# Nine checks of the adjacency matrix's entries move from VectorE in layer 1 to ScalarE under the joint sums of layers 2 and 3

## The chip, the core and the metric

The kernel runs on one core of a Trainium2 chip. Its engines are TensorE (PE, with its weight loads shown as PEld), VectorE (DVE), ScalarE (ACT), GpSimd (POOL) and SyncE (SP, which here only issues transfers). Each engine works through its own queue of instructions in the order in which the program was written; they meet only in semaphores. The metric is the device time of one execution in microseconds; the runs given here are medians. A clock of 1.00 in the profile's rows is TensorE at full speed.

## The reference

Four graph layers run over x (4096 rows of 64) and an adjacency matrix adj (4096 by 4096, f32). Each layer has the form x = x + layer(relu(layernorm(x)), adj).

```python
# layer 0: attention, masked by adj
att = adj * sigmoid((2 + 2 * (qm @ k.T)) / att_scale + att_bias);  support = att @ h
x = x + support / sqrt(|inner(support)|)
# layer 1: for each row the last 100 neighbours, weights 0.5 ** (their number from the end)
mask = (adj != 0); rank = cumsum(mask, axis=1)
x = x + w @ (h @ weight) + bias
# layer 2
x = x + 1 - 0.1 * h - 0.01 * sum(h * (adj @ h), axis=1)
# layer 3
x = x + relu(concat([h, (adj @ h) / max(deg, 1)]) @ W.T)
```

The entries of adj are drawn as 0 or 1, but nothing in the reference says that they are. The kernel has a fast path that is right only if every entry is 0 or 1, a check of every entry, and a general path that runs after the fast one where any entry is something else.

## The kernel before, in words

**Tiles.** The matrix comes transposed, cut into 8 blocks of 512 rows (ib) and 32 tiles of 128 neighbours (t). The fast path loads it once as fp8 masks, with POOL's transfers converting on the way. It is loaded a second time, in f32, only to be checked. A narrow check takes one tile (128 x 512, 0.25 MB), a wide one two (128 x 1024, 0.5 MB).

**Checks.** `fetch` (L426) issues a load on SP into the next of a ring of buffers, and `check` (L446) lets DVE count the entries that are not 0 or 1, with `(x != 0) != x` and a running sum, into one column of `odd`. A check leaves as many loads under way as `ahead` says: three in layer 1 with three buffers `ckw`, four in the joint sums, where two halves of the area of `s2a` (free once layer 1 is over) make it five buffers. Layer 0 makes 60 narrow checks, layer 1 and the joint sums together 98 wide ones.

**Layer 1** (L1490 to L1610). Masks are counted into ranks by products on PE (`cnt`, L1500), four at a time. Each result goes through a relu that gives the weights `w`, on ACT or on DVE, and the weights enter the sums (`acc`, L1535). Two blocks run together, in four groups and 66 rounds of four. A planner in the program decides which engine converts: `weights` (L1511) keeps a running estimate of when DVE and ACT come free (`Planned`, L53) and takes ACT unless it is late. Checks are paced by `due`, which grows by CHECKS_1 / 66 a round (L1446 and L1587); a check is emitted when one is due and DVE's estimate has room, or when four are due. Five more stand under the counting of the masks ahead of it. At the end of each block its sum is moved out by ACT (`asb`, L243), and `rows1` (L1314) turns it into the inputs of layers 2 and 3: norms on DVE, POOL and ACT, a transpose on PE (`ph`, L1352), its copy by ACT (`ht`, L1357), products on PE (`pn`, L1367), copies by ACT (`fa`, `v`) and a split into two fp16 parts `s` on POOL and DVE.

`rows1` and the like are generators: each `yield` is a place where other work may be emitted. `step` (L374) advances all those under way by one. So the order on every engine is fixed when the program is built.

**Joint sums of layers 2 and 3** (L1697). `both_summed` issues 1024 products of 128 x 256 (L1632), 32 for each of 32 row tiles, two tiles (a pair) at a time. The first six pairs run interleaved over the first 28 neighbour tiles, so that the last blocks of `rows1` have time to finish. After every eight products `beat` (L1615) calls `step`, and on every second beat `check(2)`, which makes 58 wide checks here. When a pair is complete, `last_rows` (L1657) finishes it: `high` on ACT, `agg`, an inner product and `y` on DVE, `xm` on ACT, `y` again on DVE, and a store. The next pair's `h` and `xm` are begun by ACT and POOL shortly before. Seven PSUM banks hold the pairs.

**The flag.** `flagged` (L1287) waits until no check is left, sums `odd` to `bad` on DVE, lets PE add up the partitions (`pf`, L1297) and DVE write a flag. Every engine reads it (L1725) before the last row tile and branches on it at the end.

Of the kernel before, what the change touches and what calls it, by code (L numbers as in the profile page):

```python
# [11 lines left out]
F32 = mybir.dt.float32  # L12
# [13 lines left out]
D = 64  # L26
# [52 lines left out]
def kernel(  # L79
# [35 lines left out]
    nc.vector.memset(one, 1.0)  # L115
    eps = cpool.tile([P, 1], F32, name="eps")
    nc.vector.memset(eps, EPS)
    eps_up = cpool.tile([P, 1], F32, name="eps_up")
    nc.vector.memset(eps_up, EPS / UP / UP)

# [46 lines left out]
    def model(general):  # L167
# [7 lines left out]
        def pool(name, bufs, on=stack, **kw):  # L175
            return on.enter_context(tc.tile_pool(name=name + sfx, bufs=bufs, **kw))
# [1110 lines left out]
        def flagged(flag):  # L1287

            steps = 7 if general else 4
            while checks or fetched:  # L1290
                yield
            bad = small("bad", "")[:, 0:1]
            dve.tensor_reduce(bad, odd, AX.X, ALU.add)
            for _ in range(steps):
                yield
            pf = pm.tile([P, CI], F32, tag="pr", name="pf")
            nc.tensor.matmul(pf[0:1, 0:1], bad, one, start=True, stop=True)  # L1297
            yield
            dve.tensor_scalar(flag, pf[0:1, 0:1], 1.0, None, ALU.min)
# [143 lines left out]

        GROUPS = ((0, 1), (2, 3), (4, 5), (6, 7))
        MOST = 120.0
        PRODUCT, ROUND, CHECKS_1 = 0.216, 1.85, 35  # L1446
        LATEST, CHECK_LATE = (1.8, 2.0, 2.2, 2.0), 1.5
        many, turns = {}, [0]

# [162 lines left out]
        SKEW = 1  # L1612
        summed, beats = [0], [0]

        def beat():  # L1615
            step()
            beats[0] += 1
            if beats[0] % 2:
                check(2)

        flag, any_odd = None, []

        LEAD, SPLIT, PAIR = 6, 28, 2
        BANKS = (2, 5, 6, 0, 1, 3, 4)
# [32 lines left out]
        def last_rows(acc, tiles, tag, begun=None):  # L1657
# [1 line left out]
            n, last = len(tiles), begun is not None  # L1659
            h, xm = begun or rows_begun(tiles, tag)  # L1660
            high, agg = (
                ends.tile([P, n, 2, D], F32, tag=a, name=f"{a}_{tag}", bufs=2)
                for a in ("high", "agg")
            )
            y = ends.tile([P, n, D], F32, tag=f"y{last}", name=f"y_{tag}", bufs=2)
            inn = ends.tile([P, n], F32, tag="inn", name=f"inn_{tag}", bufs=2)
# [65 lines left out]
        if not general:  # L1732
            with tc.manual_schedule():
                for n in range(2):
                    free = q_sb[:, n * NT // 2 : (n + 1) * NT // 2, :]
                    more.append(free.rearrange("p (c a) d -> p c (a d)", c=CG))
                ahead[0], counting[0] = 4, False
                ends = pool("ends", 1, l2)
                both_summed()
            l2.close()  # L1740
            stack.close()
            return any_odd
# [169 lines left out]
```

## Time and profile before

| | us |
|---|---|
| median of 3 runs | 573.25 (572.57 to 573.76) |
| the profiled execution | 572.18, span 569.5 |
| masks counted, then layer 1's rounds | from about 296, rounds from 311.6 |
| last product of layer 1 | starts at 443.86 |
| joint sums, first to last product | 444.08 to 563.3 |
| PE, DVE, ACT, POOL busy | 552.0, 467.5, 358.8, 272.2 |
| wide check on DVE | 1.27 mean |
| conversion of weights, ACT and DVE | 0.61 and 0.69 mean |
| load for a wide check, 0.5 MB, issue to landing | 4.3 median |

A row of the instructions in order of time gives the start, how long it took (several joined rows: from the first start to the last end), the engine, the line in the kernel, the operation with output and input, shapes and a count. A bracket gives the idle time of the engine just before the row and the instruction that ended it. Nearly all rows of DVE and ACT carry L73, the line of the helper that records them, so they are told apart by their tiles. A busy matmul's end is modelled, so a row of products is read by the distance to the next row's start: four products of layer 1 take 0.86 us without a wait, one of the joint sums 0.107. "issue to landing" is the time from SP's issue to the semaphore that says the data is there.

### The profile page before, as it was taken

How to read it: one execution, taken by the hardware profiler on the slowest of the kernel's cores; microseconds unless marked ns; L12 is line 12 of the kernel's file. 1: busy time of each engine (PE TensorE's matmuls, PEld its weight loads, DVE VectorE, ACT ScalarE, POOL GpSimd, SP SyncE). 2: the span in 40 equal slices, each digit the busy share in tenths (PEclk: the TensorE clock that was granted, in tenths of full speed). 3: DMA queues.
4: the chain of work that ended last, by engine and by line, in shares of the span. 5: the costliest groups of instructions: out<-in, count | busy, mean ns of one | idle time of the engine just before them, and what ended most of it. 6: DMA issues, size and time to landing. Idle time of an engine off the chain costs nothing.

```text
span 569.5 us, 9915 instructions
## 1 busy us (share of the span) xinstructions
PE 552.0 (97%) x3368; PEld 280.8 (49%) x3368; DVE 467.5 (82%) x949; ACT 358.8 (63%) x663; POOL 272.2 (48%) x526
## 2 busy tenths in 40 slices
PE   8999999999999999999999999999999999999995
PEld 3563333333333333333334444445454788888884
DVE  4679657799999999898976877778969897799993
ACT  3677667766676776778741888988888432342231
POOL 7624402675757576754444510384634343334332
PEclk9999999999999999999999999999999999999998
DMA  8995952689999999994223465453544788859960
GB/s 145 133 106 47 100 50 20 57 131 154 150 169 150 166 126 173 152 158 121 74 89 113 151 209 168 132 170 112 155 145 132 241 266 304 274 190 323 343 251 21
DMA packets 45612, 87.86 MB, mean 154 GB/s; under 512 B 6272, under 2 KB 24576, under 8 KB 45552
## 3 DMA queue, kind: packets, MB, share of 16 engines
q1 hardware_dynamic: 26112, 69.14, 36.5%
q0 software_dynamic: 18912, 17.77, 33.0%
q8 instruction: 28, 0.46, 0.3%
q10 hardware_dynamic: 528, 0.23, 0.2%
q14 instruction: 32, 0.26, 0.2%
HBM read 135.60 MB, written 1.05 MB: 240 GB/s over the span
## 4 chain that ended last, share of the span: by engine, by line
PE 70%; DVE 13%; POOL 5%; ACT 5%; issue 3%; DMA 2%; DVEq 0%; ACTq 0%; POOLq 0%; SPq 0%
PE acc L1090 15%; PE acc L1632 15%; PE ps L1059 15%; PE acc L1535 8%; PE cnt L1500 8%; PE idle L1183 3%; DVE att L73 3%; DVE ckw L73 2%; PE many L1387 1%; DMA s2a<-adjt_dram 1%; DVE s2a L73 1%; ACT ps L73 1%; DVE rrq L73 1%; POOL mask L211 1%; PE pt L266 1%
## 5 line engine op out<-in xcount | busy, mean ns | idle before, releaser
L1059 PE MATMUL ps<-qt,kt 64*128 64x512 f32 x512 | 123.4, 610 | 3.4 <-DVE att L73 3.0
L1090 PE MATMUL acc<-att,fb 128*64 128x512 f32 x512 | 117.8, 599 | 0.6 <-DVE att L73 0.5
L1632 PE MATMUL acc<-s,mask 128*128 128x256 f16 x1024 | 114.0, 273 | 0.4 <-DVE s L73 0.4
L73 ACT ACTIVATE w<-cnt 128x512 int16<-128x512 f32 x187 | 98.6, 606 | 12.1 <-PE cnt L1500 11.0
L1632 PEld LDWEIGHTS <-mask 128*128 128x128 fp8e4 x1024 | 99.8, 98 | 13.0 <-issue 1.0
L73 DVE TENSOR_TENSOR att<-ps,mask 128x1024 f32<-128x1024 f32 x82 | 98.6, 1217 | 8.6 <-ACT ps L73 8.5
L73 DVE SCALAR_TENSOR_TENSOR ckw<-ckw 128x1024 f32<-128x1024 f32 x76 | 96.0, 1274 | 4.2 <-DMA ckw<-adjt_dram 4.2
L73 ACT ACTIVATE ps<-ps,att_c,att_a 128x1024 f32<-128x1024 f32 x82 | 93.8, 1175 | 1.3 <-PE ps L1059 0.8
L73 ACT ACTIVATE att<-ps,att_c,att_a 128x1024 f32<-128x1024 f32 x46 | 54.6, 1202 | 54.1 <-PE ps L1059 53.9
L1059 PEld LDWEIGHTS ps<-qt,kt 64*128 64x128 f32 x512 | 44.8, 186 | 79.0 <-issue 28.7
L211 POOL DMA_DIRECT2D mask<-adjt_dram x128 | 70.1, 560 | 19.1 <-DMA mask<-adjt_dram 17.4
L73 DVE TENSOR_TENSOR att<-att,mask 128x1024 f32<-128x1024 f32 x46 | 56.9, 1252 | 18.8 <-ACT att L73 18.5
L1500 PE MATMUL cnt<-mask,after 128*128 128x512 fp8e4 x256 | 67.4, 379 | 2.7 <-DVE two L73 0.8
L1090 PEld LDWEIGHTS acc<-att,fb 128*64 128x64 f32 x512 | 33.5, 136 | 73.0 <-issue 67.6
L1535 PE MATMUL acc<-w,s2a 128*128 128x512 bf16 x256 | 66.2, 379 | 1.2 <-ACT asb L73 1.2
L73 DVE TENSOR_SCALAR w<-cnt 128x512 int16<-128x512 f32 x69 | 46.9, 686 | 22.6 <-PE cnt L1500 22.2
L301 POOL TENSOR_TENSOR rs_a<-rs_y 128x4 f32<-128x4 f32 x48 | 19.1, 398 | 67.4 <-DVE rs_y L73 61.0
L73 DVE SCALAR_TENSOR_TENSOR ck<-ck 128x512 f32<-128x512 f32 x60 | 42.8, 713 | 0.0
L1535 PEld LDWEIGHTS <-s2a 128*128 128x128 f16 x256 | 24.6, 98 | 33.6 <-issue 5.6
L1500 PEld LDWEIGHTS <-after 128*128 128x128 bf16 x256 | 24.4, 99 | 31.0 <-issue 2.7
L73 ACT ACTIVATE xm<-xm,inn 128x64 f32<-128x64 f32 x32 | 10.4, 347 | 45.9 <-DVE high L73 44.2
L1183 PE MATMUL idle<-ones 128*128 128x512 bf16 x126 | 30.9, 401 | 1.6 <-DVE ones L73 1.6
(248 smaller groups left out, 611.9 us busy)
## 6 DMA issues: line engine op xcount, KB each, us to landing
ckw<-adjt_dram SPq DMA_DIRECT2D x76, 512.0 KB, 4.3
mask<-adjt_dram POOLq DMA_DIRECT2D x128, 128.0 KB, 8.7
ck<-adjt_dram SPq DMA_DIRECT2D x60, 256.0 KB, 5.9
s2a<-adjt_dram SPq DMA_DIRECT2D x22, 512.0 KB, 4.9
x_sb<-x_dram SPq DMA_DIRECT2D x4, 256.0 KB, 7.5
out_dram<-y POOLq DMA_DIRECT2D x15, 64.0 KB, 3.7
apart_m<-mask SPq DMA_DIRECT2D x16, 16.0 KB, 4.1
mask<-apart_m SPq DMA_DIRECT2D x16, 16.0 KB, 4.3
```

Source lines behind the costliest of these rows:

```text
L73: return op(out, *args, **kw)
L211: nc.gpsimd.dma_start(out=masks[ib][:, g * CG : (g + 1) * CG, :], in_=adjt[ib, g])
L266: nc.tensor.transpose(pt[:, c, :], part, ident)
L301: nc.gpsimd.tensor_tensor(a, y, y, ALU.mult)
L1059: nc.tensor.matmul(ps[:, c, :], kt[half, g, :], qts[ib][half, :], start=True, stop=True)
L1090: nc.tensor.matmul(acc[c * D : (c + 1) * D, :], lhs[:, t, :], rhs[:, c, :], start=(at == 0), stop=(at == NG - 1), skip_group_check=True,)
L1183: nc.tensor.matmul(v.idle[:, v.filling % CG, :], ones, ones.unsqueeze(1).to_broadcast([P, IB // P, P]), start=True, stop=True, skip_group_ ...
L1387: nc.tensor.matmul(pc[q * NT : (q + 1) * NT, :], lane[:, NT - 1 - t : 2 * NT - 1 - t], masks[quad * QUAD + q][:, t, :], start=(t == 0), st ...
L1500: nc.tensor.matmul(cnt, by, what, start=True, stop=True, skip_group_check=True)
L1535: nc.tensor.matmul(accs[ib], apart_s if t < 0 else both(s2a, t), w, start=(t == NT - 1), stop=False, skip_group_check=True,)
L1632: nc.tensor.matmul(acc[:, to, :, :].rearrange("p k d -> p (k d)"), masks[ib][:, t, c * P : (c + 1) * P], s23[:, t, :, :].rearrange("p k d ...
```

## The change

Nine wide checks are handed to ACT. When the joint sums begin, 18 tiles are taken off the end of the list of checks, and a generator `tested_by_act` is advanced by one step on each beat. For each of the nine it issues a load on SP into a buffer of its own (`cka`, one buffer), waits five beats, and makes four passes over the 1024 columns, two beats apart. Each pass sums its results along the row: relu(x - 1) and relu(-x), both zero if every entry lies in 0 to 1, and sign(x) and sign(1 - x), which for 0 and for 1 add up to one and for anything between to two. The load for the next is issued on the beat after the fourth pass. One cycle is 12 beats, so the loads stand at beats 1, 13, ... 97 of 128 and the last pass at beat 108.

`flagged` waits for these too, and `oddness` folds their sums into `bad` with six small steps on DVE. In layer 1 the pace of checks goes from 35 to 26 over the rounds. `agg` goes from two buffers to one. A constant of -1 is filled at the start. By the order of the built instructions, layer 1 then makes 30 wide checks for 40 (those under the counting included), the joint sums 59 on DVE for 58 and 36 passes on ACT, `pf` stands 16 products later on PE, and two conversions of weights move from ACT to DVE; PE's other work, POOL's and the order of ACT's other work stay as they were.

```diff
         def flagged(flag):
             steps = 7 if general else 4
-            while checks or fetched:
+            while checks or fetched or not (general or tested):
                 yield
             bad = small("bad", "")[:, 0:1]
             dve.tensor_reduce(bad, odd, AX.X, ALU.add)
+            if not general:
+                oddness(bad)
...
-        PRODUCT, ROUND, CHECKS_1 = 0.216, 1.85, 35
+        PRODUCT, ROUND, CHECKS_1 = 0.216, 1.85, 26
...
         def beat():
             step()
             beats[0] += 1
             if beats[0] % 2:
                 check(2)
+            next(passes, None)
...
+        BY_ACT, FIRST_PASS = 9, 5
+        tested = []
+
+        def tested_by_act():
+            sums = ends.tile([P, 4, BY_ACT], F32, name="act_sums")
+            unused = evac.tile([P, CG * IB], BF16, tag="asb", name="act_unused", bufs=1)
+            for n in range(BY_ACT):
+                k = by_act.pop() - 1
+                by_act.pop()
+                at = ends.tile([P, CG * IB], F32, tag="cka", name=f"cka_{k}", bufs=1)
+                nc.sync.dma_start(out=at, in_=adjt[k // NT, k % NT // CG].rearrange("p c i -> p (c i)"))
+                for _ in range(FIRST_PASS):
+                    yield
+                for m, (func, bias, scale) in enumerate(
+                    ((AF.Relu, less, 1.0), (AF.Relu, 0.0, -1.0), (AF.Sign, 0.0, 1.0), (AF.Sign, one, -1.0))
+                ):
+                    nc.scalar.activation(
+                        unused, at, func, bias=bias, scale=scale, accum_out=sums[:, m, n : n + 1]
+                    )
+                    yield
+                    if m < 3:
+                        yield
+            tested.append(sums)
+
+        def oddness(bad):
+            out, signs = (small(f"act_{a}", "", ends, 1) for a in ("out", "signs"))
+            sums = tested[0]
+            dve.tensor_reduce(out, sums[:, 0:2, :], AX.XY, ALU.add)
+            dve.tensor_reduce(signs, sums[:, 2:4, :], AX.XY, ALU.add)
+            good = float(BY_ACT * CG * IB)
+            dve.tensor_scalar(out, out, 0.0, None, ALU.not_equal)
+            dve.tensor_scalar(signs, signs, good, None, ALU.not_equal)
+            dve.tensor_tensor(bad, bad, out, ALU.add)
+            dve.tensor_tensor(bad, bad, signs, ALU.add)
...
-                ends.tile([P, n, 2, D], F32, tag=a, name=f"{a}_{tag}", bufs=2)
-                for a in ("high", "agg")
+                ends.tile([P, n, 2, D], F32, tag=a, name=f"{a}_{tag}", bufs=bufs)
+                for a, bufs in (("high", 2), ("agg", 1))
...
                 ends = pool("ends", 1, l2)
+                by_act = [checks.pop() for _ in range(CG * BY_ACT)][::-1]
+                passes = tested_by_act()
                 both_summed()
```

More of the change, by code (lines that the diff above doesn't have):

```diff
@@ L117 @@
     nc.vector.memset(eps, EPS)
+    less = cpool.tile([P, 1], F32, name="less")
+    nc.vector.memset(less, -1.0)
     eps_up = cpool.tile([P, 1], F32, name="eps_up")
@@ L1613, in model @@
         summed, beats = [0], [0]
+        passes = iter(())
         def beat():
```

## The prediction, made before the changed kernel was run

> **What bounds the kernel now.** I read the page's busy row, then the busy time of layer 1 and of the joint sums in stretches of 10 us, then each engine's instructions in order of time at three places.
>
> ```profile
> PE 552.0 (97%) x3368; PEld 280.8 (49%) x3368; DVE 467.5 (82%) x949; ACT 358.8 (63%) x663; POOL 272.2 (48%) x526
> ```
>
> PE is the bound over the span, but stages differ. In the stretches (length, then PE, PEld, DVE, ACT, POOL busy, clock, DMA share, GB/s) 330 to 340 is layer 1, the others the joint sums of layers 2 and 3:
>
> ```profile
> 330.00:340.00 10.00, 10.00 (x48) 4.54 (x47) 7.63 (x13) 9.10 (x19) 0.13 (x1) 1.00 0.58 186
> ...
> 520.00:530.00 10.00, 10.00 (x94) 8.95 (x93) 9.93 (x28) 2.98 (x10) 2.75 (x4) 1.00 0.95 331
> 530.00:540.00 10.00, 10.00 (x94) 8.97 (x92) 9.97 (x24) 1.63 (x6) 4.52 (x6) 1.00 1.01 355
> ```
>
> Layer 1 has ACT as the fuller helper and DMA to spare. In the joint sums ACT is nearly free, but DVE and the DMA engines are both full. The change takes checks out of the first place and puts loads and ACT work into the second.
>
> PE in layer 1 runs four products in 0.86 us, round after round. The exceptions name who made it wait:
>
> ```profile
> 322.05 1.04 PE L1500 MATMUL cnt<-mask,after 128*128 128x512 fp8e4 x4 [0.80 <-DVE two L73]
> ...
> 345.45 0.38 PE L1535 MATMUL acc<-w,s2a 128*128 128x512 bf16 x1 [0.20 <-ACT asb L73]
> ...
> 362.90 1.35 PE L1500 MATMUL cnt<-mask,after 128*128 128x512 fp8e4 x3 [0.36 <-ACT w L73]
> ...
> 429.09 0.59 PE L1500 MATMUL cnt<-mask,after 128*128 128x512 fp8e4 x2 [0.18 <-DVE w L73]
> ```
>
> Only the first and the last end in DVE. The tail of the joint sums, DVE and then PE:
>
> ```profile
> 553.92 1.22 DVE L73 SCALAR_TENSOR_TENSOR ckw<-ckw 128x1024 f32<-128x1024 f32 x1
> 555.06 0.08 DVE L73 DVE_READ_ACCUMULATOR ckw<-ckw 128x1 f32 x1
> 555.18 0.34 DVE L73 TENSOR_REDUCE bad<-odd 128x1 f32<-128x176 f32 x1
> ```
>
> ```profile
> 556.05 0.19 PE L1297 MATMUL pf<-one,bad 128*1 128x1 f32 x2
> 556.17 7.16 PE L1632 MATMUL acc<-s,mask 128*128 128x256 f16 x64
> ```
>
> The product pf stands in PE's own queue. The sum it reads (bad) is ready at 555.52 and PE arrives at 556.05: DVE has 0.53 us to spare, and whatever it is later than that, PE stands still with 64 products to go.
>
> **The change, part by part.**
>
> *Checks out of layer 1.* By the instruction order, layer 1 loses ten wide checks and not nine (40 to 30, those under the counting among them), and the joint sums get 59 on DVE for 58. Ten at 1.15 us from start to next start are 11.5 us of DVE, but PE waits for few of them. Only two of the weights' conversions move from ACT to DVE, so the waits that end in ACT (345, 362, 377, 411) stay. At 322 the check at 319.44 stood right before the two steps PE waited for (320.58, 321.30). One check now stands there where two did, so I take 0.8 of the 0.97 us that PE lost (321.08 to 322.05). At 429 the same check stands in the same place, so its 0.34 us stay. Term: -0.8; bounds 0 and -1.3 (both waits gone).
>
> *Passes at the start of the joint sums.* The first load for ACT (cka) is issued behind a load into s2a's area, and the first pass on it stands on ACT ahead of ht of block 4, which PE needs for its product pn at 452.21.
>
> ```profile
> 450.47 0.42 ACT L73 ACTIVATE s<-fa 128x256 f32<-128x256 f32 x1 [4.61 <-POOL fa L332]
> 450.79 0.35 ACT L73 COPY ht<-ph 128x256 f32<-128x256 f32 x1
> ```
>
> ```profile
> DMA to landing us min/median/max: 8.1/8.1/8.1
> ```
>
> That last line is the load issued at 445.64, the one now just ahead of cka; its neighbours took 5.7 (445.22) and 6.5 us (448.74). PE's last product of layer 1 (443.86, ended 444.24) lets cka out at about 444.2 after the gain above, to land between 449.9 and 452.3. A pass has no row of its own. The nearest are ACT's 1024-column sigmoids, two in 2.26 us and so 1.10 apart, and the 1024-column copy, 1.01. Small passes with an accumulator start 0.24 apart. I take 1.1, between 0.95 and 1.3. So ht ends at 451.4 to 453.8 where pn wants it at 451.5: PE loses 0 to 2.3 us. Behind the waiting pass stand sq of block 6 and the copies and roots of block 5, all feeding later turns of PE; PE already waits 0.5 at 458.08 and 0.4 at 478.57, which would swallow part. Term: +0.7; bounds -0.9 (DVE's lead removes those two waits) and +2.6.
>
> *SP's queue.* Each cka waits for the fourth pass on the one before, since there is one buffer, and DVE's own loads queue behind it. On DVE's side four loads are out at a time, so a hold of 2 us costs nothing while they last. But ACT's lateness is handed on: the first load's last two passes follow the root kept (455.35 now, about 457.5 behind late copies) and end at 460; the second load lands at 465 and its last pass follows the root rs of block 7 (472.37 now, 473.6 then), ending at 474.7; the third lands at 480 and its last pass follows the copies of block 7 (481.82 to 482.6 now, 484.2 then), ending at 485.3. That puts the load of cka_248 at 485.4, to land at 489.8 (4.4 to 4.8 us there). Its first pass stands ahead of h and high of pair 0 (1.02 us), so DVE's agg of that pair starts at about 492 instead of 489.32, and all DVE's checks behind it are as late. DVE has 3.4 us of waits for stores (DMA out_dram) before 510 that may take some back. Term: +1.2; bounds 0 and +2.6.
>
> *Passes under a full DVE.* From 515 on DVE runs 6.25 us a pair (agg at 540.27 and 546.53) with no gap, PE 6.83 (64 products of 0.107), so DVE catches up 0.58 a pair. Loads land in 5.2 to 5.4 us with a DMA share near 1. Work out pair 8 to 9 in the new order: the fourth pass on cka_244 ends 1.4 (xm) + 3.3 (three passes) = 4.7 us after agg of pair 7; the next load lands 5.3 later, 3.75 after agg of pair 8; two passes, h and high end at 3.75 + 2.2 + 1.02 = 6.97, where agg of pair 9 wants it at 6.25. DVE idles 0.7. In pairs 7 and 10 the first pass stands ahead of xm: its load goes out after xm and one pass of the pair before (1.4 + 1.1 = 2.5) and lands 5.3 later, 7.8 us after that pair's agg, that is 1.55 into the pair, pass and xm end at 3.25, y wants it at 2.28: 0.97. With 0.95 us a pass and loads of 5.0 these become 0.55 and 0.4. Two of each, between 1.9 and 3.3; with each lateness handed to the next load, up to 5.1; none if ACT's idle 4.72 us a pair holds them. Term: +2.4, from inside the first two; bounds 0 and +5.1.
>
> The Trainium skill's page "DMA: Bandwidth & Descriptors" (Issuing engines are not separate DMA queues; Specifications) says that all issuers share the same 16 engines and puts HBM at about 358 GB/s a core. By it 4.67 loads of 0.524 MB a pair take 6.84 us for DVE's 6.25, an estimate of 0.6 a pair over six pairs: 3.5 us in place of this term. The page "ScalarE: Activation LUTs" (Rules for kernel authors) says relu and its like belong on VectorE, which speaks against the change; its cost formula would make a pass about 1.0 us, and the term an estimate of 2.1.
>
> *The tail.* One more check (1.15), y moved ahead (0.2) and six small steps of the signs' sums (starts 0.2 apart, as in DVE's inn steps at 308: 1.2) stand before bad, while pf moves 16 products later (1.71): 0.53 + 1.71 - 2.55 = -0.3. Term: +0.3, bounds 0 and 0.6. The loading of the flag by each engine (0.5 us) has then 1.7 us of products on PE to hide under; it ended 2.1 us after pf before (558.2), so I leave it at nothing.
>
> *At nothing:* agg with one buffer in place of two (DVE writes and reads it, in order), the fill of "less" at the start (DVE waits for input there).
>
> DVE's lateness ends in pf, so its terms add: -0.8 + 0.7 + 1.2 + 2.4 + 0.3 = **+3.8 us**. Against the profiled execution's own 572.18 (span 569.5 and 2.7 around it) that is 575.98. This execution is 1.07 below the median of the runs, so on the median 573.25 + 3.8 = **577.05**.
>
> **The rivals.** *The cover holds (no change):* ACT has 4.7 us idle a pair and loads have slack of a cycle; then only -0.8 and +0.3 remain, 572.75. Against it: DMA share 0.95 to 1.01. *DVE's ease wins (faster):* all PE waits that end in DVE, 0.97 at 321, 0.34 at 429 and 0.9 at 458 and 478, go, and bad is in time: 573.25 - 2.2 + 0.3 = 571.35. It decides at pf: if DVE is less than 1 us later than now at the last pair, it is this. *Both ends at their upper bounds (slower still):* first load 8 us, each late load handed on: +2.6 + 2.6 + 5.1 + 0.6 - 0.8 = 583.35 at most, about 581 likely. *Sign is in another table:* the trace's loads of a table cost 1.28 us; two for each of nine tiles are 23 us of ACT, 2.6 more per 10 us, and by the sum for pair 8 to 9 DVE idles 1.3 to 2.6 more a pair: about 585. For it: no Sign in the trace; against: Relu, Copy, Square and Sqrt share one from 362 on.
>
> **How the numbers follow.** Forecast 0.59, cover 0.12, faster 0.12, upper ends 0.13, table 0.04. About 0.2% (1.15 us) is what a measurement of this kernel can tell from no change. Range 572.1 to 581.5: it leaves out the faster case and the top of the slowest. Its own range of the forecast is 574.4 to 580. Slower 0.76, within 0.12, faster 0.12.
>
> **What would show it.** Layer 1 no longer waits 0.8 for two; PE waits for ht of block 4 behind the first cka pass; DVE waits for ACT's high and xm between 510 and 545, with loads landing later than 5.4; PE waits for bad before pf, and the last stretch after it is 48 products. Wrong if pf does not wait, if cka lands within 5 us throughout, or if the joint sums' PE time is unchanged.

## The result, and the profile after

The changed kernel takes 581.66 us, the median of five executions (580.93 to 582.87); the kernel before, timed beside it, takes 572.57 (571.90 to 573.76). The ratio is 1.0154, with a 95% interval from 1.0139 to 1.0169: the change makes the kernel 1.5% slower, some 9 us. Below, medians and ratios are reckoned apart and can differ by up to 0.24%; kernels are compared by their ratios to the kernel before, and 0.1% is 0.57 us. A trace is of one execution, and where that one is the shortest or the longest of its kernel, it is said.

The profiled execution of the changed kernel (582.80 us) has a span of 581.1 us, 11.6 more than before. The page's row of busy time, from PE to POOL:

```profile
PE 553.8 (95%) x3368; PEld 281.7 (48%) x3368; DVE 458.4 (79%) x940; ACT 397.0 (68%) x733; POOL 267.6 (46%) x526
```

PE's busy time grew by only 1.8 us and DVE's fell by 9.1, so what is new is standing still. PE's instructions in order of time show where (start, length, the instruction, and in brackets the idle time before it with who ended it):

```profile
314.09 1.94 PE L1504 MATMUL cnt<-mask,after 128*128 128x512 fp8e4 x7 [1.13 <-DMA mask<-two]
...
429.02 0.59 PE L1504 MATMUL cnt<-mask,after 128*128 128x512 fp8e4 x2 [0.18 <-DVE w L73]
...
453.82 0.71 PE L1371 MATMUL pn<-wln_sb,ht 64*128 64x128 f32 x8 [1.61 <-ACT ht L73]
...
479.29 2.56 PE L1677 MATMUL acc<-s,mask 128*128 128x256 f16 x22 [0.28 <-DVE s L73]
...
567.83 0.19 PE L1301 MATMUL pf<-one,bad 128*1 128x1 f32 x2 [9.25 <-DVE bad L73]
567.95 6.79 PE L1677 MATMUL acc<-s,mask 128*128 128x256 f16 x48
```

The wait for `two` near 322 is gone, the one for `mask` at 314 is 1.13 where it was 0.41 at 312, the one at 429 stayed, `pn` now waits 1.61 for `ht` behind the first pass on `cka`, and one row dwarfs the rest: 9.25 us for `bad`, with 48 products still to go. The steps add up: the counting began 0.95 later (that part of the kernel is untouched), from there to the end of layer 1 147.2 us in place of 148.2 (-1.0), from there to the long row of products of the joint sums 38.4 in place of 37.6 (+0.8), that row up to `pf` 85.40 in place of 74.34 (+11.1, of which 9.25 are the wait and 1.7 the 16 products by which `pf` stands later), and the rest 13.27 in place of 13.45 (-0.2). The 0.95 lie ahead of the changed parts, so this pair of traces is further apart than the medians are.

The last part deserves a look: with 16 products less to do it should have been 1.7 shorter. Its 48 products took 6.79 us; in the kernel `passes_only` below, where PE does not wait, they take 5.41. In these stretches of the changed kernel (length, busy PE, PEld, DVE, ACT, POOL, granted clock, DMA share, GB/s) the clock falls while PE waits, and stays low when it starts again:

```profile
559.00:562.00 3.00, 0.00 (x0) 0.00 (x0) 3.00 (x6) 0.99 (x4) 2.26 (x3) 1.00 0.87 284
562.00:565.00 3.00, 0.00 (x0) 0.00 (x0) 2.97 (x10) 1.48 (x5) 0.00 (x0) 0.83 0.10 41
565.00:568.00 3.00, 0.17 (x3) 0.14 (x4) 2.93 (x13) 0.41 (x2) 1.95 (x5) 0.50 0.07 22
568.00:571.00 3.00, 3.00 (x17) 2.17 (x17) 1.21 (x9) 1.05 (x3) 1.07 (x3) 0.53 0.01 3
571.00:574.00 3.00, 3.00 (x30) 2.70 (x28) 0.95 (x5) 0.63 (x2) 0.03 (x1) 1.00 0.17 45
```

So the wait cost its 9.25 us and 1.4 more: 17 products in three microseconds where 30 fit later. The Trainium skill's page "TensorE: Matmul & The Clock Gate" (Part 1: The HAM clock gate) says the clock halves after an idle window of about 3.4 us and comes back after about as long of work; here it falls some 5 us after PE stopped at 558.6, and is back some 3 us after PE starts again. In `cka_act` below, a wait shorter than the page's window brought it down too: 1.96 us on `pn`, followed by a clock of 0.50 from 483.75 to 487.16.

DVE's end of the joint sums, where `bad` is made:

```profile
565.23 1.22 DVE L73 SCALAR_TENSOR_TENSOR s2a<-s2a 128x1024 f32<-128x1024 f32 x1
566.38 0.08 DVE L73 DVE_READ_ACCUMULATOR s2a<-s2a 128x1 f32 x1
566.49 0.34 DVE L73 TENSOR_REDUCE bad<-odd 128x1 f32<-128x176 f32 x1
...
567.32 0.45 DVE L73 TENSOR_TENSOR bad<-bad,act_signs 128x1 f32<-128x1 f32 x1
```

`bad` begins at 566.49, and 555.18 before. Was DVE given more to do, or did it wait more? The same columns, from the start of the joint sums to the beginning of `bad`, first of before, then of after:

```profile
444.20:480.00 35.80, 34.84 (x321) 30.25 (x319) 31.56 (x67) 11.61 (x59) 12.80 (x16) 1.00 0.85 274
480.00:515.00 35.00, 35.00 (x324) 31.14 (x322) 28.40 (x88) 13.18 (x42) 12.68 (x24) 1.00 0.75 252
515.00:555.18 40.18, 40.18 (x370) 36.02 (x369) 39.91 (x107) 10.96 (x35) 13.56 (x18) 1.00 0.86 307
```

```profile
444.20:480.00 35.80, 33.91 (x313) 29.60 (x312) 30.03 (x63) 22.02 (x77) 12.45 (x15) 1.00 0.85 279
480.00:515.00 35.00, 35.00 (x324) 31.14 (x323) 22.38 (x73) 19.48 (x54) 8.61 (x18) 1.00 0.76 269
515.00:566.49 51.49, 43.58 (x400) 38.82 (x397) 47.79 (x127) 33.62 (x80) 14.74 (x26) 0.98 0.84 317
```

DVE's busy time is 99.9 us before and 100.2 after. Its idle time (length less busy) is 4.2 + 6.6 + 0.3 = 11.1 before and 5.8 + 12.6 + 3.7 = 22.1 after. All 11 us are waiting, and 6.0 of them arise between 480 and 515, where DVE had gaps before too. DVE's waits in that stretch (who waited for whom, us in total, times, longest), first of before, then of after:

```profile
DVE y L73 <- DMA out_dram<-y: 3.4, 4, 2.2
DVE s L73 <- POOL s L286: 1.6, 1, 1.6
DVE agg L73 <- ACT high L73: 1.6, 1, 1.6
```

```profile
DVE y L73 <- DMA out_dram<-y: 6.9, 3, 2.7
DVE agg L73 <- ACT high L73: 3.4, 1, 3.4
DVE ckw L73 <- DMA ckw<-adjt_dram: 1.1, 1, 1.1
DVE s L73 <- POOL s L288: 0.7, 1, 0.7
```

The wait for `high` grew by 1.8 and the waits for the stores of `y` by 3.5. ACT's side of it, in order of time: it stands at the fourth load, with `h` and `high` of the first pair behind the pass.

```profile
489.69 1.15 ACT L1647 ACTIVATE act_unused<-cka,less 128x1024 bf16<-128x1024 f32 x1 [5.24 <-DMA cka<-adjt_dram]
490.74 0.18 ACT L1647 ACTIVATION_READ_ACCUMULATOR act_unused<-cka,less 128x1 f32 x1
490.83 0.76 ACT L73 ACTIVATE h<-x_sb,kept,kept 128x64 f32<-128x64 f32 x2
491.50 0.36 ACT L73 ACTIVATE high<-acc 128x256 f32<-128x256 f32 x1
```

And pieces of the chain that ended last (start, length, what): a load of `cka`, its passes, a store of `y`, another store, and then load after load.

```profile
484.47 5.13 DMA cka<-adjt_dram
...
500.03 6.39 DMA out_dram<-y
...
509.98 4.04 DMA out_dram<-y
...
518.59 3.39 DMA cka<-adjt_dram
...
527.31 6.07 DMA cka<-adjt_dram
...
539.48 3.26 DMA cka<-adjt_dram
...
548.07 4.91 DMA cka<-adjt_dram
```

### The profile page after: what moved, and what is told of

The parts are those of the page before. It is cut to its first block, busy times and chain, and to the rows that moved or that the text cites. A ratio compares the mean times of both kernels' runs of the same rounds, so it can differ in the third digit from the quotient of the medians.

```text
span 581.1 us, 9970 instructions
## 1 busy us (share of the span) xinstructions
PE 553.8 (95%) x3368; PEld 281.7 (48%) x3368; DVE 458.4 (79%) x940; ACT 397.0 (68%) x733; POOL 267.6 (46%) x526
## 3 DMA queue, kind: packets, MB, share of 16 engines
HBM read 135.60 MB, written 1.05 MB: 235 GB/s over the span
## 4 chain that ended last, share of the span: by engine, by line
PE 52%; DVE 16%; ACT 10%; DMA 9%; POOL 6%; issue 5%; ACTq 0%; DVEq 0%; SPq 0%; POOLq 0%
PE acc L1092 12%; PE ps L1061 11%; PE acc L1539 9%; PE cnt L1504 9%; DMA cka<-adjt_dram 5%; DVE att L73 4%; ACT act_unused L1647 4%; PE idle L1185 3%; DVE ckw L73 2%; DMA out_dram<-y 2%; PE acc L1677 2%; DVE s2a L73 2%; PE many L1391 1%; POOL mask L213 1%; DMA mask<-adjt_dram 1%
## 5 line engine op out<-in xcount | busy, mean ns | idle before, releaser
L1677 PE MATMUL acc<-s,mask 128*128 128x256 f16 x1024 | 115.3, 275 | 0.3 <-DVE s L73 0.3
L1677 PEld LDWEIGHTS <-mask 128*128 128x128 fp8e4 x1024 | 100.5, 99 | 13.4 <-issue 0.9
L73 DVE SCALAR_TENSOR_TENSOR ckw<-ckw 128x1024 f32<-128x1024 f32 x66 | 82.4, 1259 | 6.0 <-DMA ckw<-adjt_dram 6.0
L1061 PEld LDWEIGHTS ps<-qt,kt 64*128 64x128 f32 x512 | 44.8, 186 | 79.2 <-issue 29.5
L73 DVE TENSOR_SCALAR w<-cnt 128x512 int16<-128x512 f32 x71 | 48.3, 688 | 30.9 <-PE cnt L1504 30.6
L73 DVE SCALAR_TENSOR_TENSOR s2a<-s2a 128x1024 f32<-128x1024 f32 x23 | 28.8, 1257 | 0.0
```

Of the source, the lines that this page charges most:

```text
L73: return op(out, *args, **kw)
L1061: nc.tensor.matmul(ps[:, c, :], kt[half, g, :], qts[ib][half, :], start=True, stop=True)
L1677: nc.tensor.matmul(acc[:, to, :, :].rearrange("p k d -> p (k d)"), masks[ib][:, t, c * P : (c + 1) * P], s23[:, t, :, :].rearrange("p k d ...
```

## The experiments

The theory at the start: `bad` is late because loads of `cka` and ACT's passes form a loop. ACT stands at a load that has not landed, with `h` and `high` behind it; the passes that follow are late; and the next load goes out only behind the fourth of them, since there is one buffer. Its rivals: the 4.7 MB of extra loads alone (the DMA engines are full), ACT's 44 us of passes alone, or the order of things around `pf`. All diffs are against the changed kernel unless another is named.

### Which part costs: neither, one, the other, or loads that nobody reads

`drop9` keeps the lighter layer 1 and drops the nine tiles:

```
-                passes = tested_by_act()
+                tested.append(None)
...
-            if not general:
-                oddness(bad)
```

> This kernel keeps the lighter layer 1 (30 wide checks for 40) and leaves the nine wide checks that ACT would make out of the computation: no load of cka, no pass on ACT, no sums of signs. So it has what the change takes away and nothing of what it adds to ACT and the queues. Theory (the loads and passes are what costs, and DVE's lateness ends at pf): in the trace of the changed kernel the stretch from the first tile of the counting to layer 1's last product is 147.1 us for 148.2 before, so the time is 1.0 us under the kernel before, 571.6 for 572.6, between 570.8 and 572.6, and PE waits less than 0.5 us for bad before pf. Rival (lighter layer 1 is no gain by itself, or the 59th check on DVE and the other place of pf cost): 573 to 575, with a wait before pf of 1 us or more.

571.05 us (median), ratio 0.9971 (0.9947 to 0.9995): the theory's side. So layer 1 is worth some 1.7 us, with an interval from 0.3 to 3.0. The profiled execution happened to be the longest of ten (575.64), so its wait before `pf`, 3.06, speaks for that one alone. But six of the ten lie at 570.2 to 571.2 and four at 573.8 to 575.6: without any tile on ACT, too, DVE is late in some executions. In the traced one it stood idle for 9.9 us between 480 and 515, 6.2 of them at stores of `y`.

`loads_only` lets each pass read one column of the 1024:

```
                     nc.scalar.activation(
-                        unused, at, func, bias=bias, scale=scale, accum_out=sums[:, m, n : n + 1]
+                        unused[:, 0:1], at[:, 0:1], func, bias=bias, scale=scale,
+                        accum_out=sums[:, m, n : n + 1],
                     )
```

> The nine loads of cka stay, and so do four instructions of ACT for each in the same places; but each reads one column of the 1024, so that ACT's time of 1.05 to 1.14 us a pass falls away and the nine tiles are not tested in full (that part of the computation is left out). ACT still waits for each landing ahead of h and high, and SP's next cka still waits for the fourth pass. Theory (loads and passes are a loop: a pass late by ACT's own work makes the next load late, and that the next h and high): without 4.2 us of passes a cycle the loop has room, PE waits 1 to 4 us before pf in place of 9.25, and the time is 572.5 to 576. Rival A (DMA engines full, 0.95 to 1.01 from 515 on, 4.7 MB more to move): the wait before pf stays at 6 us or more, time 578 or more. Rival B (ACT's time alone): no wait before pf, time as without the nine tiles, within 0.5 us.

578.36 us, ratio 1.0065 (1.0042 to 1.0088), and PE waits 6.77 us before `pf`. This is above the theory's range, and in rival A's numbers (the trace is of the longest of five, 580.83). Passes need not be long for the loads to hurt.

`passes_only` loads one tile and passes over it 36 times:

```
+                if n == 0:
                     at = ends.tile([P, CG * IB], F32, tag="cka", name=f"cka_{k}", bufs=1)
                     nc.sync.dma_start(...)
```

> One cka is loaded at the start, and all 36 passes read that one tile: ACT's time stays, eight loads of 0.5 MB and every wait of ACT for a landing after the first go (eight of the nine tiles are not tested: that part of the computation is left out). Theory (the loop of loads and passes): ACT has 4.72 us idle in a pair of 6.25 us and the passes of a pair take about 2.6 us by the measured 1.25 a pass, so ACT is late by less than 1 us at any h, PE waits under 2 us before pf, and the time is 571.6 to 574. Rival A (DMA full): same numbers, since it has the loads gone. Rival B (ACT's time alone makes h, high and xm late): the wait before pf stays at 6 us or more, time 578 or more.

571.90 us, ratio 0.9980 (0.9950 to 1.0009), no wait before `pf`, as the theory had it. DVE's idle time is what it was before but for 1.5 us at the start, in waits for ACT's `rs`, although ACT works for 74 us in these stretches, where it had 36. The three stretches of `passes_only` up to its `bad`:

```profile
444.20:480.00 35.80, 33.90 (x314) 29.60 (x312) 30.04 (x64) 22.80 (x80) 12.44 (x15) 1.00 0.81 270
480.00:515.00 35.00, 35.00 (x324) 31.13 (x322) 28.32 (x88) 23.62 (x62) 13.21 (x24) 1.00 0.72 258
515.00:555.81 40.81, 40.81 (x376) 36.58 (x375) 40.53 (x111) 28.01 (x65) 13.29 (x20) 1.00 0.86 312
```

ACT's time by itself is out: it costs 0.09%, half a microsecond, over the kernel without the tiles.

`loads_unread` issues the nine loads and reads none of them (the four activations are taken out, the places where they stood stay).

> Nine loads of cka are issued in the same places and into the same buffer, but nothing reads them: no pass and no small instruction on ACT, no wait for a landing there, and SP waits for no pass before it issues the next (the nine tiles are not tested: that part of the computation is left out). With the loads and one column a pass the kernel took 578.36 and PE waited 6.77 us before pf; without loads and passes it took 571.05. Theory (ACT, which works in order, stands at a cka that has not landed, 21.9 us in all there, and h and high behind it come late): with no reader the loads cost little, 571 to 573, and DVE waits for ACT's high no longer than in the kernel without the nine tiles (6.1 us in all). Rival A (the DMA engines are full, and any extra 4.7 MB make DVE's own loads and y's stores late): 575 or more, the wait before pf 3 us or more, with DVE's waits for ckw, s2a and out_dram grown.

574.03 us, ratio 1.0019 (0.9983 to 1.0054), between the two. The four executions spread from 571.43 to 576.23, and the trace is of the shortest, so it may show less waiting than the others had. There DVE's waits for `high` in the whole of the joint sums are 4.4 us (after: 7.4), as the theory had it. The bare loads cost 1.0019 - 0.9971, some 2.8 us, but the intervals of these two overlap. They land in 6.6 us at the median (after: 4.4), and the loads of DVE's checks, into `ckw` and `s2a`, in 5.6 and 5.7 (5.1 and 4.7 in `drop9`). So rival A has a part, and the larger part needs someone who stands at the loads: 2.6 us more when ACT does little at each (`loads_only`), 7.7 more with whole passes (after). That it takes both, loads and passes that read them, is shown by these four kernels; by what chain it takes both is the question of the next two sections.

| | loads | passes | ratio to before | DVE idle: 444-480, 480-515, 515 to bad | PE's wait before pf |
|---|---|---|---|---|---|
| before | - | - | 1 | 4.2, 6.6, 0.3 | 0 |
| `drop9` (longest of ten) | - | - | 0.9971 | 4.1, 9.9, 0.7 | 3.06 |
| `passes_only` | one | full | 0.9980 | 5.8, 6.7, 0.3 | 0 |
| `loads_unread` (shortest of four) | nine | - | 1.0019 | 4.4, 6.2, 2.2 | 1.29 |
| `loads_only` (longest of five) | nine | one column | 1.0065 | 5.2, 11.3, 2.0 | 6.77 |
| after | nine | full | 1.0154 | 5.8, 12.6, 3.7 | 9.25 |

### Which wait: ACT's at the landing, or SP's at the buffer

In the changed kernel ACT stood 19.9 us at landings, and SP 14.3 us after 480 at a `cka` whose buffer was in use, with DVE's loads behind it. Each is taken away once. `cover` gives the load eight beats to land and puts the passes at the last four:

```
-        BY_ACT, FIRST_PASS = 9, 5
+        BY_ACT, FIRST_PASS = 9, 8
...
                     yield
-                    if m < 3:
-                        yield
```

> Loads, passes and sums stay whole; only the places change: the load of cka at the first of twelve beats as before, the four passes at beats 9 to 12 one after the other and not at 6, 8, 10 and 12. So a load has 8 beats, 8 times 0.857 us or 6.9 us, to land in place of 4.3, and its landing took 3.2 to 7.7. Theory (ACT's standing at the landing is the cost): ACT's waits for cka fall from 19.9 us in all to under 8, PE's wait before pf from 9.25 to 0 to 5, and the time is 573 to 577.5; what is left comes from four passes of 1.25 us that stand in 3.4 us of beats ahead of h and high. Rival A (DMA engines full): wait before pf 8 us or more, time 580 or more.

583.17 us, ratio 1.0182 (1.0142 to 1.0222), and PE waits 9.94 before `pf`: no better, against the theory's 573 to 577.5. Time and wait are those of rival A, but full DMA engines alone cannot be it, by `loads_unread`: the same loads cost 2.8 us there. Yet the wait that it was to take away did go. The idle time of ACT at `cka`, then SP's queue and DVE, of `cover` after 480:

```profile
  DMA cka<-adjt_dram: 4.8, 3
```

```profile
SPq L1641 <- ACT act_unused L1647: 15.9, 5, 4.9
SPq L1641 <- ACT xm L73: 4.5, 1, 4.5
```

```profile
DVE y L73 <- DMA out_dram<-y: 6.3, 4, 2.5
DVE ckw L73 <- DMA ckw<-adjt_dram: 4.8, 5, 1.9
DVE agg L73 <- ACT high L73: 3.7, 3, 1.7
```

ACT's 15 us at landings turned into 6 more of SP at the buffer (20.4 for 14.3) and into DVE's waits for its own checks.

`cka_act` takes SP's wait away: ACT issues the loads.

```
-                nc.sync.dma_start(out=at, in_=adjt[k // NT, ...
+                nc.scalar.dma_start(out=at, in_=adjt[k // NT, ...
```

> The loads of cka are issued by ACT and not by SP, in the same places of the program; so SP, which stood 14.3 us after 480 at a cka whose buffer was still being read (20.4 in the kernel with the passes at the end of the twelve beats), goes on with DVE's own loads. ACT issues the next cka right behind its fourth pass. Theory (what is held in SP's queue is a large part of the lateness): DVE's waits for ckw go under 1 us, loads of checks and of cka no longer wait for one another, time 575 to 579. Rival (ACT's own standing at a landing, 19.9 us, ahead of h and high is what counts; issuing loads costs ACT besides): 580 to 584, with DVE's waits for high as large as before.

587.18 us, ratio 1.0253 (1.0231 to 1.0275), worse than the rival's range. With SP free to send DVE's loads, `cka` lands in 6.2 us at the median for 4.4, and ACT stands 29.0 us at it; DVE's waits for `high` ahead of `bad` are 10.5 us for 5.3. The Trainium skill's page "DMA: Bandwidth & Descriptors" (Issuing engines are not separate DMA queues) says that transfers run on the same 16 engines and interleave, whichever engine started them, and the longer landings agree with that.

So neither wait is the cause by itself; whichever is taken away, the other grows. What the three kernels share is the loop. From the first load's issue to the ninth's it goes round eight times in 103.6 us in the changed kernel, 103.8 in `cover` and 106.2 in `cka_act`. In `loads_unread`, where the loads stand at the same places and nothing reads them, it takes 94.2. The issues of the loads, in us, show where the difference arises:

| load | 1 | 2 | 3 | 4 | 5 | 6 | 7 | 8 | 9 |
|---|---|---|---|---|---|---|---|---|---|
| after | 444.49 | 459.13 | 474.54 | 484.47 | 497.43 | 518.59 | 527.31 | 539.48 | 548.07 |
| `loads_unread` | 443.29 | 455.30 | 467.90 | 477.95 | 489.16 | 507.04 | 517.84 | 527.63 | 537.52 |

The changed kernel loses 10.4 us up to the sixth load, and none behind it: its last three rounds take 29.5 us, those of `loads_unread` 30.5. An estimate of a round from the medians is 11.6 us: the landing (4.4), four passes that start 1.17 to 1.26 apart (4.9), and the rows' work that ACT does in between, `h` 0.66, `high` 0.27 and `xm` 0.5 for each of some 1.6 pairs (2.3). Twelve beats of PE in the long row of products are 10.3 us. But the last three rounds, at 9.8 each, do fit into twelve beats, with landings of 3.3 to 6.1. So the loop falls behind while ACT still has the last blocks of `rows1` and the first six pairs to serve, and later it only fails to make that up: the ninth load stands at the ninety-seventh beat, which PE passed at about 537.2 (25 beats ahead of `pf`'s turn at 558.6), and was issued at 548.07. That the one buffer is what makes the loop late is argued and not shown; a second buffer was not tried.

### Where it turns into DVE's idle time: the stores of y, and the stretch from 480 to 515

`y3` gives `y` of the pairs a third buffer:

```
-            y = ends.tile([P, n, D], F32, tag=f"y{last}", name=f"y_{tag}", bufs=2)
+            y = ends.tile([P, n, D], F32, tag=f"y{last}", name=f"y_{tag}", bufs=1 if last else 3)
```

> The changed kernel with three buffers for y of the pairs in place of two (the last two single tiles share one); all loads, passes and checks stay. In the changed kernel DVE stood idle for 12.6 us between 480 and 515, for 6.6 us before, and 6.9 us of that are waits for stores out of y's two buffers (3.4 before). Theory (the stores, late because POOL waits for ACT's h ahead of them, are half of the lump): those waits fall under 2 us, PE waits 4 to 6 us before pf in place of 9.25, time 576 to 579. Rival (the store's wait only stands where another wait would: high, xm or a load of checks): DVE's idle time stays within 1.5 us of 12.6 with other names in it, and the time within 1.5 us of the changed kernel, 580 to 583.

577.90 us, ratio 1.0076 (1.0052 to 1.0100), a wait of 5.28 before `pf`: the theory's numbers, 4.5 us off the changed kernel's time though all loads and passes are there. The trace names no wait of DVE for stores any more (2.5 us ahead of `y` behind 515 have no name in it), and its idle time from 480 to 515 is 5.4, less than before; a part of that came back behind 515, where 3.7 became 6.4. The stretches of `y3`:

```profile
480.00:515.00 35.00, 35.00 (x324) 31.13 (x323) 29.62 (x90) 22.78 (x62) 12.78 (x24) 1.00 0.86 296
515.00:561.51 46.51, 42.56 (x390) 37.90 (x388) 40.15 (x108) 29.27 (x68) 10.94 (x20) 0.99 0.86 322
```

The starts of `agg` on DVE, less those of the same pair before (us), show how the lateness grows:

| pair | 0 | 3 | 4 | 6 | 7 | 9 | 13 |
|---|---|---|---|---|---|---|---|
| after | 2.57 | 2.99 | 5.83 | 7.50 | 7.04 | 9.08 | 9.96 |
| `loads_only` | 0.61 | 3.95 | 4.14 | 5.80 | 5.33 | 6.19 | 6.97 |
| `passes_only` | 0.01 | -0.21 | -0.02 | -0.10 | 0.08 | -0.32 | -0.72 |
| `y3` | 1.83 | 0.34 | 0.53 | -0.20 | -0.67 | 1.20 | 4.98 |

The changed kernel is 2.57 late at the first pair, for the load that ACT stood at, and that stays to pair 3. Then 2.8 come at pair 4 and 2.2 more at pair 6, behind stores, and from pair 9 on a little more with each load. With a third buffer the first 1.83 are made up by pair 3: DVE can run ahead where stores do not hold it. The kernel before was not tried with three buffers, so how much of the 4.5 us a third buffer would bring without the change is open. DVE's waits for stores were 2.7 to 3.4 us in the profiles of before, `passes_only` and `loads_unread`, 6.3 to 7.1 in those of after, `loads_only`, `cover` and `pf_late`, and 6.2 in the longest execution of `drop9`: they vary on their own too. Nor are they needed for a late end: `cka_act`, the slowest kernel, has 3.3 of them and no growth of lateness between pairs 0 and 7 (3.6 and 4.0), and gets its lateness (13.4 at pair 13) behind 515, where DVE waits 7.0 us for `high`.

`pause7` leaves the stretch alone:

```
-        PRODUCT, ROUND, CHECKS_1 = 0.216, 1.85, 26
+        PRODUCT, ROUND, CHECKS_1 = 0.216, 1.85, 28
-        BY_ACT, FIRST_PASS = 9, 5
+        BY_ACT, FIRST_PASS = 7, 5
...
+                if n == 3:
+                    for _ in range(24):
+                        yield
                 k = by_act.pop() - 1
```

> Seven wide checks by ACT for nine, the other two back in layer 1 (32 there for 30); no load and no pass between the third tile and the sixty-first beat, so that the stretch from 485 to about 503, in which the first six pairs come due at once, has none. All is computed. Theory (that stretch is where most of the lateness arises: DVE's idle time there was 12.6 us against 6.6): it falls to 6 to 8, PE waits 2 to 4.5 us before pf, time 574 to 577.5. Rival (each tile costs alike, wherever it stands): 7/9 of 9.1 us, 579 to 580.5.

576.70 us, ratio 1.0084 (1.0064 to 1.0104); DVE's idle time from 480 to 515 is 5.8 and PE waits 4.21 before `pf`. The theory's numbers came, all of them: two tiles fewer of nine took away 4 us of some 9, twice what they would by count. One thing beside the pause helped: the first load landed in 5.8 us for 7.7, at another pace of the checks ahead of it, and `pn` did not wait (1.61 in the changed kernel). And behind 515 DVE's idle time is 4.4 for 3.7, so the pause took away the lateness of the stretch and not that of the full DVE.

### How it reaches the end: pf's place

`pf_late` puts `pf` 40 products later, and the loading of the flag behind the last tile:

```
-            steps = 7 if general else 4
+            steps = 7 if general else 9
...
-                        if j == 0:
+                        if j == 1:
                             any_odd.append(nc.values_load(flag[0:1, 0:1], min_val=0, max_val=1))
```

> The changed kernel with the product pf five beats (40 products, 4.3 us) later in PE's order, and the loading of the flag behind the products of the last tile. Nothing in front of pf changes. Theory (DVE's lateness reaches the end only through pf's place): PE waits 9.25 less 4.3, about 5 us, and has 8 products left behind it; the granted clock, which was 0.5 to 0.53 for some 6 us after the wait of 9.25, falls for less long; the time is 575.5 to 579. Rival (the end goes through DVE's last rows, y and their stores, which stand behind bad on DVE, or through the loading of the flag, now at the end): within 1.5 us of the changed kernel, 580 to 583.

579.55 us, ratio 1.0114 (1.0092 to 1.0136), just past the theory's 579. PE waits 5.09, as it should (the trace is of the longest of four). But only 2.3 us come off the time: the eight products behind `pf` take 1.89 us, 0.24 each for 0.107 at full clock, and the last tile's `high` on ACT now waits 1.3 us for the flag. So the rival has some of it.

`act9_pace35` leaves nine tiles to ACT but gives layer 1 its 40 checks back (`CHECKS_1` 35), so that DVE has 49 in the joint sums.

> The passes and loads stay whole, but layer 1 keeps its 40 wide checks, so the joint sums have 49 on DVE for 59: the same loop, with 11.5 us of DVE taken off ahead of pf. Theory (the nine tiles cost PE nothing but through bad before pf, and 0.7 us at the start of the joint sums): DVE gets 10 times 1.15 us back, pf is not waited for, and the time is the one of before plus 0.5 to 1, 573 to 574. Rival (the passes or loads make PE itself wait in the joint sums, or delay y and its stores at the end, whatever DVE's checks do): 576 or more, with waits on PE other than pf after 480.

581.07 us, ratio 1.0108 (1.0064 to 1.0153): the rival's time, but by waits that neither side saw. (Two executions took 578.7 and 578.9, two 583.2 and 583.8; the trace is of the longest.) PE waits 4.40 before `pf`, in a place 64 products earlier, since `pf`'s place follows from where checks and passes run out. `bad` did come 6.6 us earlier (559.9), but DVE's idle time up to it is 25.8 us, more than in the changed kernel: fewer checks leave the loop as it is, eight rounds in 103.8. The first load, here sent at 447.6 and landed at 456.6, cost PE 4.47 us at `ht`, for 1.61.

### Other ways to do it

`pace26_dve` is the kernel before with the lighter layer 1, and leaves the checks to DVE, with one check more in each twelve beats (twelve, where the expectation has six):

```
-        PRODUCT, ROUND, CHECKS_1 = 0.216, 1.85, 35
+        PRODUCT, ROUND, CHECKS_1 = 0.216, 1.85, 26
...
-            if beats[0] % 2:
+            if beats[0] % 2 or beats[0] % 12 == 6:
```

> The kernel before with the lighter pace in layer 1 (30 wide checks for 40), and the ten wide checks that this leaves over made by DVE in the joint sums, one more in every six beats; nothing on ACT, agg with two buffers. Theory (in the joint sums DVE is full from 515 on, so each check moved there comes out at pf): ten at 1.15 us less the 0.53 us by which bad is early, 11 us of wait before pf, less 1.0 in layer 1, plus 1 to 2.5 of slow clock after the wait: 582 to 586, so that the move to ACT saved 1 to 4 us against leaving the checks on DVE. Rival (DVE's waits in the joint sums, some 13 us, take the checks up): 574 to 579, and the move to ACT was dearer than no move.

584.23 us, ratio 1.0196 (1.0172 to 1.0219), within the theory's range; the wait before `pf` is 7.49 and not 11, and another of 2.57 stands at 478 (the trace is of the shortest of four). So moving the nine to ACT saved 2.4 us against moving them within DVE.

`three` leaves ACT three tiles, 36 checks in layer 1, and time to land:

```
-        PRODUCT, ROUND, CHECKS_1 = 0.216, 1.85, 26
+        PRODUCT, ROUND, CHECKS_1 = 0.216, 1.85, 32
-        BY_ACT, FIRST_PASS = 9, 5
+        BY_ACT, FIRST_PASS = 3, 12
...
+            for _ in range(40):
+                yield
             for n in range(BY_ACT):
...
                     yield
-                    if m < 3:
-                        yield
+                    yield
+                    yield
```

> Only three wide checks by ACT, 36 in layer 1; the first load at the forty-first beat, behind the start of the joint sums and with 12 beats (10.3 us) to land, the passes three beats apart, so that SP never stands at a buffer and ACT at no landing. All is computed. Theory (passes themselves cost nothing, and loads cost little when nobody stands at them): layer 1's gain of 1.0 stays, bad is late by less than 1 us, 571 to 573.2. Rival (the extra loads fill the DMA engines, three at 9.1/9 each): 574.5 or more.

572.70 us, ratio 0.9998 (0.9983 to 1.0014), inside the theory's 571 to 573.2. ACT stands at no landing and SP at no buffer, and the 1.5% is gone. Not that `bad` is always in time: the trace is of the longest of twelve (576.85), and PE waits 5.32 before `pf` in it, with 5.1 of DVE's waits between 480 and 515 at stores. And it is no faster than before: what layer 1 gains is lost again, to the three loads perhaps, which no run shows. None of the kernels that compute everything beats the one before.

## Why the prediction was right, and where its sizes were wrong

The direction and the place were right: `pf` waits for `bad`, and 48 products follow. The size was not: the forecast was +3.8 us (577.05, of its own 574.4 to 580), and some 9 came. The measured time (a median of 581.66, or 581.4 by the ratio to the kernel timed beside it) is at the top end of the whole range, 572.1 to 581.5, where one of the rivals stood. Of the terms:

- *Checks out of layer 1*, -0.8: the wait at 322 went and the one at 429 stayed, as written. Of the waits that end in ACT, the one at 377 (0.34) went too, against the prediction, and the wait for `mask` at 314 grew by 0.7, for which it had no term. Measured -1.0 in the profile; `drop9` puts the whole of it at -1.7 (-3.0 to -0.3), and in its trace a further 0.9 comes off at the start of the joint sums (36.7 us to the long row, 37.6 before).
- *Passes at the start of the joint sums*, +0.7: `pn` waits 1.61 for `ht` behind a first pass that begins at 452.27, and the waits at 458 (0.53, gone) and 478 (0.43, now 0.28) shrink. Measured +0.8 against before, and 1.7 against `drop9`.
- *SP's queue*, +1.2 with an upper bound of 2.6: this is the step that failed, by its size. Its working up to the first pair was right to the tenth, `agg` of pair 0 at "about 492" was at 491.89, 2.57 later than before. But the term is smaller than that, since it said that DVE's 3.4 us of waits for stores may take some back. They grew to 6.9 in the trace instead, and DVE's idle time from 480 to 515 rose by 6.0. A late start in a row of pairs that share two buffers of `y` was not made up; `y3` shows that with a third it is.
- *Passes under a full DVE*, +2.4 with a bound of 5.1: DVE's idle time behind 515 rose by 3.4, in the waits that were named (for `high` 0.9 twice) and in waits for loads of its own checks, 1.3 and 0.2. So the term was a little small and within its bound; it did not need a loop that gets slower there, and the last three rounds, at 9.8 us each, show none.
- *The tail*, +0.3: from the first step of `bad` to `pf` it is 1.3 us, 1.0 of them for the six small steps that were put at 1.2. The rest of the term could not be seen apart from the wait.
- *Left out altogether*: PE's slow clock behind a long wait, 1.4 us.
- *At nothing*: `agg` with one buffer shows no wait on DVE in the waits above, and `drop9`, which keeps the one buffer, is not slower than the kernel before.

Of the rivals, *the cover holds* and *DVE's ease wins* both decided at `pf`, and fell there by 9 us. *Both ends at their upper bounds* named about 581 and got the number, though not by its division and so partly by luck: start 0.8 and not 2.6, the second and third term together 9.4 of DVE's idle time. *Sign in another table* fell: ACT loads a table four times, before and after. The estimate from the Trainium skill's page "DMA: Bandwidth & Descriptors" (Specifications), 3.5 us by 358 GB/s a core, is near what the bare loads cost (2.8), but not by that limit: `loads_only` moved 403 GB/s from 530 to 540.

```profile
530.00:540.00 10.00, 10.00 (x94) 8.96 (x93) 8.86 (x21) 3.64 (x16) 4.16 (x6) 1.00 1.02 403
```

The rule of the Trainium skill's page "ScalarE: Activation LUTs" (Rules for kernel authors), that relu and its like belong on VectorE, would have given the right sign here for another reason than the one measured: the passes' own time cost 0.5 us.

## What to carry to other kernels

Idle time on an engine is no cover for work that waits: 44 us of passes over a tile that lay ready fitted into ACT for half a microsecond, and with a load behind each set of four the kernel was 10 us slower, of which the bare loads explain some 3. Before moving work into a loop with one buffer, add up one round (landing, work, and what its engine does in between), hold it against the time the program gives it, and do so for each stage: here the loop fell behind early and kept up later. Moving the wait to another queue did not help in either of two tries. And ask of every row of work with few buffers whether a late start can be made up there.

## What the runs showed of the hardware that was not expected

- A wait of PE costs more than its length. Behind no wait or one of 1.29 us, 48 products took 5.41 us; behind waits of 3.06, 4.21, 5.28, 6.77 and 9.25 they took 7.08, 6.91, 7.72, 8.07 and 6.79. It does not grow with the wait: 1.4 to 2.7 us for any of 3 us or more. Waits of 1.96 us (`cka_act`, at 483) and 2.57 us (`pace26_dve`, at 478) were followed by 3.4 us at a clock of 0.50 as well; waits of 1.6 at the start of the joint sums left it at 1.00.
- A pass over 1024 columns takes 1.05 us, 1.14 with its bias from memory, and the sum read out behind it 0.187 more; even a pass of one column is 0.19, or 0.28 to 0.30 with its bias from memory, and 0.187.
- Loads that nobody reads still go with slower landings of the others: with nine of them DVE's own took 5.6 and 5.7 us at the median, without them 5.1 and 4.7 (one trace each, `loads_unread` and `drop9`).
